# Queries and keys by seven half-size products instead of eight, with the message products moved

## The chip, the cores and the metric

The kernel runs on one core of a Trainium2 chip. The metric is the device time of one execution in microseconds (us), given as the median over the executions of a run. Engines: PE is TensorE's matmuls, PEld its weight loads, DVE is VectorE, ACT is ScalarE, POOL is GpSimd.

## The reference, cut to what matters

Two graph-attention layers on 64 graphs of 256 nodes with 512 features, all in fp32. The part concerned is in layer 0:

```python
m = embs @ map_w.T + map_b                       # 256 x 512 per graph
...
q = (m @ q_w.T + q_b)                            # 256 x 512, 8 heads of 64
k = (m @ k_w.T + k_b)
scores = einsum('bhsd,bhtd->bhst', q, k) / sqrt(64)
...
sem_h = (embs @ gcn_map_w.T + gcn_map_b)         # the "messages"
Ax = einsum('hbst,hbtd->hbsd', adj_h, sem_h)
```

(... cut: normalization, cosine threshold, softmax, layer 1.)

## The kernel before

Each graph goes through a software pipeline, one *period* per graph, in which layer 0 of graph i, layer 1 of graph i-1 and the preparation of graphs i+1 and i+2 are interleaved by hand. The order in the program is the order of each engine's queue; TensorE's timelines below show its products in that order.

```python
def features_first(wt, src, ms, name):
    p = bank(name)                                # one PSUM bank of a ring of 8
    nk = wt.shape[1]                              # 4 chunks of 128
    for n, m in enumerate(ms):
        for c in range(nk):
            nc.tensor.matmul(p[:, n, :], wt[:, c, m * P:(m + 1) * P], src[:, c, :],   # 128 x 256
                             start=(c == 0), stop=(c == nk - 1))
    return p

def queries(g, n):                                # keys: the same with wk, bk, kT
    ...
    p = features_first(w.wq, g.mT, (2 * n, 2 * n + 1), f"p_q{g.i}_{n}")
    for k in range(2):
        m = 2 * n + k
        nc.scalar.activation(g.qT[:, m, :], p[:, k, :], AF.Identity, bias=w.bq[:, m:m + 1])

def messages(g, t):
    ...
    for c in range(NKC):
        nc.tensor.matmul(p, g.hT[:, c, t * P:(t + 1) * P], w.wc[:, c, :], ...)          # 128 x 512
    nc.vector.tensor_add(g.sem[:, t, :], p, w.bc)

def period(i):                                    # g: graph i, b: i-1, nx: i+1, n2: i+2
    ...                                           # scores of g, mapped(nx), cosines, layer-1 scores of b
    if g:
        far_off(g, 2, co[2])                      # VectorE: a <- co, e; GpSimd: e + a, halves
        far_off(g, 3, co[3])
    if nx:
        messages(nx, 0)
        messages(nx, 1)
    if n2:
        edges(n2)
        moments(n2, f"0_{n2.i}")
    if nx:
        queries(nx, 0)
        queries(nx, 1)
    ...                                           # values, sums, division, result 0 of b, heads_back(g)
    if nx:
        lengths(nx, p_n)
        keys(nx, 0)
    ...                                           # moments, deviations, normalized of g (layer 1)
    if nx:
        ...
        keys(nx, 1)
    if g:
        hT = turned(g, f"1_{i}")                  # p_t: waits for VectorE's xn
    ...
```

## Time and profile before

| what | before |
|---|---|
| time, median | 4105.03 us (4103.81 to 4105.85, 4 runs) |
| one period (steady, from the starts of p_m) | 63.05 or 63.06 us, 60 times of 61 |
| TensorE busy / clock granted (share of full clock) | 99% / 0.998 |
| queries + keys per graph, start to next start | 7.00 + 6.94 = 13.94 us |
| messages per graph | 6.97 us |

Lines of a profile group instructions by program line, engine, operation and tile. These two are the heaviest users of the weight loader in the change (busy us, mean ns of one, then the idle time before them and what ended it):

```profile
L191 PE MATMUL p_q<-mT,wq 128*128 128x256 f32 x2048 | 452.7, 379 | 0.0
L191 PEld LDWEIGHTS p_q<-mT,wq 128*128 128x128 f32 x2048 | 389.0, 190 | 80.1 <-issue 30.5
```

An fp32 matmul leaves two records, so 64 graphs x 16 matmuls are 2048. The matmuls never waited (0.0). The 379 ns are a record's latency, not its pitch; the pitch is 7.00/32 = 0.219 us (0.216 from record to record, and 0.309 once, from the last one to av, whose tiles are 128*64 and not 128*128), and the loads run beside the matmuls: 31 of the 32 loads of queries lie in the 6.67 us from 2027.79, inside the 7.00 us of their matmuls.

### The profile page before, as it was taken

The page shows a single profiled execution, that of the slowest core. Times are in us where ns is not written, and L with a number is a line of the kernel's source. Part 1 is how long each engine was busy: PE and PEld are TensorE (multiplying, and loading weights), DVE is VectorE, ACT ScalarE, POOL GpSimd, SP SyncE. Part 2 cuts the span into 40 slices and gives each one's busy share as a digit, 9 for nine tenths or more (in the row PEclk, how much of TensorE's full clock was granted, in tenths as well). Part 3 has the DMA queues.
Part 4 walks back from the last instruction along what each step waited for, and adds up shares of the span by engine and source line. Part 5 has one row for each costly group of instructions (what it writes and reads, how often), then busy time and mean ns, then how long its engine had stood idle before and what let it go on. Part 6 is the DMA issues. An engine that isn't in the chain of part 4 may idle for free.

```text
span 4102.0 us, 56638 instructions
## 1 busy us (share of the span) xinstructions
PE 4050.7 (99%) x23649; PEld 3072.0 (75%) x23649; DVE 2233.5 (54%) x3160; ACT 1453.2 (35%) x3010; POOL 1559.9 (38%) x1030
## 2 busy tenths in 40 slices
PE   8999999999999999999999999999999999999997
PEld 6777777777777777777777777777777777777775
DVE  3555555555555555555555555555555555555553
ACT  2333333333333333333333333333333333333332
POOL 2334344243343343443433434434334344343341
PEclk9999999999999999999999999999999999999999
DMA  2000000000000000000000000000000000000000
GB/s 88 12 23 12 23 23 12 22 13 22 23 12 23 23 12 23 15 19 23 12 23 22 12 23 17 18 23 12 22 23 12 23 17 18 23 12 23 23 6 17
DMA packets 56517, 81.59 MB, mean 20 GB/s; under 512 B 21888, under 2 KB 21888, under 8 KB 56256
## 3 DMA queue, kind: packets, MB, share of 16 engines
q1 hardware_dynamic: 52224, 71.32, 5.3%
q0 software_dynamic: 1760, 6.55, 0.4%
q8 instruction: 188, 3.08, 0.3%
q14 instruction: 73, 0.60, 0.0%
q10 hardware_dynamic: 2272, 0.04, 0.0%
HBM read 44.34 MB, written 33.55 MB: 19 GB/s over the span
## 4 chain that ended last, share of the span: by engine, by line
PE 91%; DVE 6%; ACT 1%; issue 0%; DMA 0%; POOL 0%; ACTq 0%; POOLq 0%; DVEq 0%
PE p_q L191 16%; PE p_k L191 16%; PE p_m L191 11%; PE p_s L231 11%; PE sc L280 8%; PE p_o L389 6%; PE co L280 6%; PE p_v L476 5%; DVE rz L382 5%; PE av L308 3%; PE p_t L181 3%; PE p_b L251 2%; PE zb L375 1%; PE p_l L356 1%; DVE oT L384 1%; ACT z L378 1%
## 5 line engine op out<-in xcount | busy, mean ns | idle before, releaser
L315 POOL TENSOR_TENSOR e<-e,a 128x1024 f32<-128x1024 f32 x252 | 654.7, 2598 | 1649.9 <-DVE a L295 1649.9
L288 DVE TENSOR_TENSOR e<-e,mask 128x1024 f32<-128x1024 f32 x384 | 563.8, 1523 | 164.6 <-ACT e L287 164.6
L301 POOL TENSOR_TENSOR d<-e 128x512 f32<-128x512 f32 x378 | 528.7, 1413 | 42.9 <-DVE e L288 23.1
L255 DVE TENSOR_TENSOR nT<-mT,p_b 128x512 f32<-128x512 f32 x128 | 82.2, 684 | 713.3 <-PE p_b L251 713.3
L191 PE MATMUL p_m<-hT,wm 128*128 128x256 f32 x2048 | 461.0, 383 | 0.7 <-ACT hT L182 0.7
L231 PE MATMUL p_s<-wc,hT 128*128 128x512 f32 x1024 | 456.5, 599 | 0.0
L191 PE MATMUL p_k<-mT,wk 128*128 128x256 f32 x2048 | 452.8, 379 | 0.0
L191 PE MATMUL p_q<-mT,wq 128*128 128x256 f32 x2048 | 452.7, 379 | 0.0
L191 PEld LDWEIGHTS p_q<-mT,wq 128*128 128x128 f32 x2048 | 389.0, 190 | 80.1 <-issue 30.5
L191 PEld LDWEIGHTS p_m<-hT,wm 128*128 128x128 f32 x2048 | 385.2, 191 | 72.1 <-ACT e L287 20.5
L382 DVE RECIPROCAL rz<-z 128x512 f32<-128x512 f32 x64 | 214.6, 3353 | 406.1 <-ACT z L378 406.1
L191 PEld LDWEIGHTS p_k<-mT,wk 128*128 128x128 f32 x2048 | 384.2, 190 | 49.6
L287 ACT ACTIVATE e<-sc 128x512 f32<-128x512 f32 x768 | 389.7, 617 | 84.6 <-PE sc L280 83.9
L263 ACT ACTIVATE qT<-p_q,bq 128x256 f32<-128x256 f32 x256 | 107.5, 470 | 867.6 <-PE p_q L191 867.6
L360 POOL TENSOR_TENSOR xs<-xs,o 128x512 f32<-128x512 f32 x128 | 159.8, 1270 | 580.1 <-DVE o L358 580.1
L231 PEld LDWEIGHTS p_s<-wc,hT 128*128 128x128 f32 x1024 | 189.3, 190 | 235.2 <-issue 234.5
L295 DVE SCALAR_TENSOR_TENSOR a<-co,e 128x512 f32<-128x512 f32 x512 | 317.0, 679 | 11.4 <-PE co L280 11.4
L389 PE MATMUL p_o<-wo,oT 128*128 128x512 f32 x512 | 248.3, 608 | 15.4 <-DVE oT L384 15.3
L463 POOL TENSOR_TENSOR xs<-xs,bo_b 128x512 f32<-128x512 f32 x128 | 170.6, 1351 | 222.8 <-DVE xn L172 219.1
L280 PE MATMUL co<-nT 64*128 64x256 f32 x2048 | 251.4, 384 | 1.2 <-DVE a L295 1.2
L476 PEld LDWEIGHTS p_v<-wv,hT 128*128 128x128 f32 x1024 | 194.5, 190 | 54.1 <-ACT hT L182 15.5
L476 PE MATMUL p_v<-wv,hT 128*128 128x256 f32 x1024 | 231.6, 379 | 0.4 <-ACT hT L182 0.4
(113 smaller groups left out, 5443.8 us busy)
## 6 DMA issues: line engine op xcount, KB each, us to landing
xs<-in_x_dram SPq DMA_DIRECT2D x64, 512.0 KB, 3.8
out_dram<-xs SPq DMA_DIRECT2D x64, 512.0 KB, 2.8
ad<-in_adj_dram SPq DMA_DIRECT2D x64, 64.0 KB, 3.6
wm<-in_L_gnn_map_w_dram POOLq DMA_DIRECT2D x1, 1024.0 KB, 9.1
gw<-in_L_gnn_gcn_map_w_dram POOLq DMA_DIRECT2D x2, 512.0 KB, 10.0
wq<-in_L_gnn_q_w_dram POOLq DMA_DIRECT2D x1, 1024.0 KB, 13.8
wk<-in_L_gnn_k_w_dram POOLq DMA_DIRECT2D x1, 1024.0 KB, 16.4
wv<-in_L_gnn_Wv_dram POOLq DMA_DIRECT2D x1, 512.0 KB, 18.0
```

Of the source, the lines that this page charges most:

```text
L191: nc.tensor.matmul(p[:, n, :], wt[:, c, m * P:(m + 1) * P], src[:, c, :], start=(c == 0), stop=(c == nk - 1))
L231: nc.tensor.matmul(p, g.hT[:, c, t * P:(t + 1) * P], w.wc[:, c, :], start=(c == 0), stop=(c == NKC - 1))
L280: nc.tensor.matmul(ps[s][:, j, :], rows[h, c, j * P:(j + 1) * P], cols[h, c, :], start=True, stop=True)
L287: nc.scalar.activation(e[:, s, :], p.rearrange("p j q -> p (j q)"), AF.Exp, scale=SCALE)
L288: nc.vector.tensor_mul(e, e, mask[:, None, :].to_broadcast([P, 2, NT * S]))
L295: nc.vector.scalar_tensor_tensor(q[:, s, :], p.rearrange("p j q -> p (j q)"), THRESHOLD, e[:, s, :], op0=ALU.is_gt, op1=ALU.mult)
L301: nc.gpsimd.tensor_add(d, e[:, :, :S], e[:, :, S:])
L315: nc.gpsimd.tensor_add(g.e[c], g.e[c], g.q[c])
L382: nc.vector.reciprocal(rz, b.z)
L389: nc.tensor.matmul(p, b.oT[:, c, t * P:(t + 1) * P], w.wo1[:, c, :], start=(c == 0), stop=(c == NIC - 1))
L463: nc.gpsimd.tensor_add(g.xs[:, t, :], g.xs[:, t, :], w.bo_b)
L476: nc.tensor.matmul(p[:, t, :], hT[:, c, t * P:(t + 1) * P], w.wv1[:, c, :], start=(c == 0), stop=(c == NKC - 1))
```

## The change

The intent: Strassen's identity (in Winograd's form with shared sums) computes a product of 2x2 blocks by seven block products instead of eight. The blocks are 256 x 256 of weights and 256 features x 128 tokens of mT, so the products run in 128-column matmuls. Sums of mT blocks are made by GpSimd, the weight blocks once at the start. The products accumulate in PSUM where the identity allows. The message products go behind the sums, into the places that the keys had. To make room, several tiles lose their second buffer.

```diff
+    def left_factors(src, name):
+        a = [src[:, HC * k:HC * (k + 1), t * P:(t + 1) * P] for t in range(2) for k in range(2)]
+        ss = sb1.tile([P, 4, HC, P], F32, tag="wide", name=f"ss{name}")
+        nc.gpsimd.tensor_add(ss[:, 0], a[2], a[3])
+        nc.gpsimd.tensor_sub(ss[:, 1], ss[:, 0], a[0])
+        nc.gpsimd.tensor_sub(ss[:, 2], a[0], a[2])
+        nc.gpsimd.tensor_sub(ss[:, 3], a[1], ss[:, 1])
...
+    def seven_products(left, wt, bias, dst, name):
+        pa = bank(f"{name}_a", [P, 2, HC, P])          # two halves of one bank
+        pb = bank(f"{name}_b", [P, 2, HC, P])
+        pc = bank(f"{name}_c", [P, HC, P])
...                                                     # product(): 4 matmuls of 128 columns; biased(): 2 ScalarE copies
+        product("a", pa[:, 0], 1, a12)
+        p2 = biased(pa[:, 0], 0, 2, bufs=1)
+        product("a", pa[:, 1], 0, a11)
+        out(0, 0, pa[:, 1], p2)                        # VectorE
+        yield
+        product("c", pc, 6, a22)
+        p4 = biased(pc, 0, 4)
+        yield
+        product("b", pb[:, 0], 3, s1)
+        p5 = biased(pb[:, 0], 1, 5)
+        product("b", pb[:, 1], 2, s4)
+        yield
+        product("a", pa[:, 1], 4, s2)
+        u4 = sb1.tile([P, HC, P], F32, tag="uu", name=f"uu{name}")
+        nc.vector.tensor_add(u4, pa[:, 1], p5)
+        out(0, 1, pb[:, 1], u4)
+        yield
+        product("a", pa[:, 1], 5, s3)
+        out(1, 1, pa[:, 1], p5)
+        out(1, 0, pa[:, 1], p4)
...
+    def queries_and_keys(g):
+        ...
+        for step in (q, k, q, q, k, q, k, k, q, k):
+            next(step, None)
...
         if nx:
-            messages(nx, 0)
-            messages(nx, 1)
+            queries_and_keys(nx)
         if n2:
             edges(n2)
             moments(n2, f"0_{n2.i}")
-        if nx:
-            queries(nx, 0)
-            queries(nx, 1)
...
             lengths(nx, p_n)
-            keys(nx, 0)
+            messages(nx, 0)
...
-            keys(nx, 1)
+            messages(nx, 1)
```

(Cut: the loading of four weight blocks and the making of seven, eight VectorE subtractions at the start; tiles hT, sem, rn, adb from two buffers to one, xn from four to two; the sums and the tile avs, which share one place; the messages of the first graph, now ahead of its products; the slow path for unusual inputs, which does not run here.)

Names used below: P1 and P2 are the products of weight blocks 0 and 1, the first to be issued; p_q_a, p_q_b, p_q_c are q's three PSUM banks and p_k_a to p_k_c those of k; u2, u4, u5 are ScalarE's copies of products with the bias added. A *turn inside a bank* is: a product into one half of a bank, ScalarE's copy out of that half, the next product into the other half.

## The prediction

> **What bounds the kernel now.** I read the page first (busy shares, the chain that ended last), then one period of the tensor engine's timeline, then the vector engine's timeline in the same stretch.
>
> ```profile
> PE 4050.7 (99%) x23649; PEld 3072.0 (75%) x23649; DVE 2233.5 (54%) x3160; ACT 1453.2 (35%) x3010; POOL 1559.9 (38%) x1030
> ...
> PE 91%; DVE 6%; ACT 1%; issue 0%; DMA 0%; POOL 0%; ACTq 0%; POOLq 0%; DVEq 0%
> ```
>
> TensorE is busy 99% and is 91% of the chain: it issues almost without a gap, so a microsecond saved there is a microsecond saved, and any new gap there is added in full. The timeline of TensorE shows a period of 63.05 us per graph (the query matmuls start at 1964.73 and again at 2027.78), 64 graphs in all. The parts that the change touches:
>
> ```profile
> 2018.99 1.89 PE L280 MATMUL co<-nT 64*128 64x256 f32 x16
> 2020.81 7.13 PE L231 MATMUL p_s<-wc,hT 128*128 128x512 f32 x16
> 2027.78 7.07 PE L191 MATMUL p_q<-mT,wq 128*128 128x256 f32 x32
> 2034.78 1.95 PE L308 MATMUL av<-e,v 128*64 128x256 f32 x16
> ...
> 2042.65 1.96 PE L389 MATMUL p_o<-wo,oT 128*128 128x512 f32 x4 [0.17 <-DVE oT L384]
> ...
> 2045.75 7.07 PE L191 MATMUL p_k<-mT,wk 128*128 128x256 f32 x32
> 2052.69 1.07 PE L181 MATMUL p_t<-ident,xn 128*128 128x128 f32 x8
> ```
>
> Columns: start, length, engine and line, operation, count. One fp32 matmul leaves two records. From start to next start queries take 7.00 us and keys 6.94 us, 0.216 us per record of 256 columns: 13.94 us per graph. Messages (p_s) take 6.97. No bracket on p_s, p_q, p_k: they wait for nothing. What the other engines do behind them:
>
> ```profile
> 2019.44 4.24 DVE L288 TENSOR_TENSOR e<-e,mask 128x1024 f32<-128x1024 f32 x2 [0.36 <-ACT e L287]
> ...
> 2023.60 2.47 DVE L295 SCALAR_TENSOR_TENSOR a<-co,e 128x512 f32<-128x512 f32 x4
> 2026.00 0.68 DVE L232 TENSOR_TENSOR sem<-p_s,bc 128x512 f32<-128x512 f32 x1
> ```
>
> VectorE is behind: TensorE left the cosine products (co) at 2020.81, VectorE finishes with them at 2026.0, 5.2 us later. Now this costs nothing, because messages and queries ask VectorE for nothing in that time.
>
> The price of a half-width record stands at the start of the run, where weights are folded by 128-column fp32 matmuls:
>
> ```profile
> L108 PEld LDWEIGHTS p_wc<-gt,gw x32: 192/192/192, 27.8 to 31.2; 128*128 128x128 f32 x32
> L108 PE MATMUL p_wc<-gt,gw x32: 275/275/275, 27.9 to 31.4; 128*128 128x128 f32 x32
> ```
>
> The timeline puts 32 loads in 3.65 us with the last one's 0.19: (3.65-0.19)/31 = 0.112 us per record.
>
> [...] the masking of e takes 1.16 us each at 2008.29 (4.63 for 4, GpSimd idle) and 2.12 at 2019.44 (GpSimd busy).
>
> **The change part by part.**
>
> 1. Matmul work. Seven products of 2x2 blocks, 28 matmuls of 128 columns instead of 16 of 256, for q and for k: 112 records x 0.112 = 12.5 us instead of 13.94. Saved: 1.4 us per graph, 92 us in all, 2.2%. The arithmetic fell by an eighth, weight loads rose from 64 to 112, and the records got 4% dearer per column. This is the whole possible gain.
>
> 2. Turns inside a bank. I read the built program's waits engine by engine. Three times per graph the order on TensorE is: product into half of a bank; ScalarE copies that half out with bias (two 128x128 instructions); the very next product goes to the other half of the same bank and waits for that copy. This is so for P2 then P1 of q, and for blocks 3 then 2 of q and of k. Nothing stands between. One turn: a record lasts 275 ns at a pitch of 112, so 0.16 until it has ended; 0.04 to ScalarE's start (p_q ended 2034.85, its copy began 2034.89); two copies,[...] 0.63; 0.1 back to TensorE (oT ended 2042.50, p_o began 2042.65); 0.1 for the exposed load of the first record (377 against 275 ns in p_bc). Together 1.0 us, three times: +3.0.
>
> 3. The fourth turn, P2 then P1 of k, is worse. ScalarE's copy of k's P2 has a single buffer (u2) with q's, so it first waits until VectorE has added q's P1 and P2; and that add stands on VectorE after all four a<-co pairs, which end 5.2 us after TensorE starts on q. From there: add 0.42 (as rn<-p_n, 0.41), 0.04, copies 0.63, back 0.1: TensorE can go on at 6.4. It reaches this wait after three products of 0.89, one turn of 1.0 and 0.1 for the change of array tiling: 3.8. Stall +2.6. The four GpSimd operations of the left factors (about 0.73 each, half of 128x512's 1.27 to 1.41 plus its fixed part, 2.9 us from 2016.4) stand before e<-e,a and push it to 2019.3, where VectorE's masking wants to begin;[...] VectorE ends 0.5 to 1.6 us later. I take +0.9, so +3.5.
>
> 4. Later products: those that accumulate into a region that VectorE has read (blocks 4 and 5) have one or two products of 0.89 between, against about 0.65 for the read and its two hand-overs: no stall. VectorE's ten adds per graph, 4.2 us, are otherwise beside TensorE.
>
> 5. Messages in place of keys fill 6.97 instead of 6.94: nothing. But their evacuation moves from ScalarE to VectorE's queue, ahead of the statistics for layer 1. p_s of token tile 0 ends about 3.7 us after p_l, VectorE's add 4.4, statistics 1.9 more, square root, reciprocal, first xn at about 7.5; TensorE arrives at 7.0. Now p_t waits 0.1 on average. +0.4.
>
> 6. p_o stays as it is: z, rz, oT shift with TensorE, and the statistics of graph n+2 are done before z. Single buffers for hT, sem, rn, adb and two for xn: each next writer comes after the last reader in TensorE's own order, no wait. Seven weight blocks at the start, 8 subtractions and longer first products: +4 us once.
>
> Sum per graph: -1.4 +0.1 +3.0 +3.5 +0.4 = +5.6, less a little where the turns overlap; I take +5.4. 63 x 5.4 + 4 = 344; 4105 + 344 = 4449, rounded to 4445 us.
>
> **The rivals.** (a) The gain comes through: if the waits inside a bank were already met when TensorE comes there, 4105 - 92 + 25 (p_t) = 4040 us. For it: the author interleaved q and k in order to hide the turns. Against it: three turns have no product between, and the order of the queues is fixed. (b) Only the short turns count, because VectorE is less late than I think: -1.4 + 0.1 + 4.0 + 0.4 = +3.1, about 4305. Against it: the 5.2 us of lag stand alike at 1957.76, 2020.81 and in the next period. (c) GpSimd becomes a drag: left factors plus contention delay VectorE by the full 1.6 or more, +6.3 and over, 4510. (d) Weight loads become the bound and a record costs more than 0.112: each 0.01 more is 1.1 us per graph, 70 us.
>
> **Range and chances.** The turns are certain in kind; their size (0.8 to 1.2) moves the total by 25 either way, VectorE's lag at the fourth turn by 60, p_t by 25, the record pitch by 20. Range 4345 to 4530. Faster by over 2% needs (a) in full, 3%; within 2% 4%; slower 93%.
>
> **What the profile after would show.** TensorE's busy share falls to about 92% or less (busy time nearly as now or lower), with idle before the product line put down to ScalarE, three times about 1 us and once about 3 us per graph; that one preceded by ScalarE waiting for VectorE. Record pitch in the products near 0.112. Masking of e on VectorE as slow as now or slower. A small idle before p_t put down to VectorE's xn. A period of about 68.5 us. I am wrong if TensorE has no gaps in the products, or if the long gap is missing, or if a large new gap stands at p_o.

Of the sum, two stand without their reasons: in part 2 the 0.63 us of the two copies (0.16 + 0.04 + 0.63 + 0.1 + 0.1 = 1.03, taken as 1.0), and in part 3 the +0.9, with the 0.5 to 1.6 us behind it. The sum: -1.4 + 0.1 + 3.0 + 3.5 + 0.4 = +5.6 per graph, taken as +5.4; 63 x 5.4 + 4 = 344; 4105 + 344 = 4449, put as 4445 us. The changed kernel's trace has the copies at 0.63 us, the four sums on GpSimd at 0.73 each, and the +0.9 at 0.27 in most periods (below).

## The result

| | before | after |
|---|---|---|
| time, median | 4105.03 us (4 runs) | 4487.45 us (4468.53 to 4494.38, 4 runs) |
| ratio | 1 | 1.0925 (95%: 1.0891 to 1.0958) |
| period, most frequent | 63.06 us | 68.07 or 68.08 us |
| queries + keys | 13.94 us in two pieces | 18.68 us in one piece |
| clock granted | 0.998 | 0.988 (0.984 to 0.988 in four runs) |

A ratio is the mean time of one kernel's fast runs over that of the other's of the same rounds, so it is not quite the ratio of the medians. The change made the kernel 9% slower; the predicted 4445 us (4345 to 4530) was 42 us too low and its range holds. All outputs are right.

The page of the changed kernel, busy shares and the chain that ended last:

```profile
PE 4077.0 (91%) x26721; PEld 3157.7 (71%) x26721; DVE 2366.5 (53%) x3805; ACT 1486.0 (33%) x3266; POOL 1745.2 (39%) x1292
...
PE 73%; POOL 14%; DVE 7%; ACT 2%; issue 2%; POOLq 0%; DVEq 0%; ACTq 0%
```

TensorE is no longer 91% of the chain, and GpSimd stands in it with 14%. Its timeline in one ordinary period (start us, length us, what; in brackets the idle time before and who ended it):

```profile
2004.50 1.16 PE L238 MATMUL p_q_a<-mT,wq 128*128 128x128 f32 x8
2006.38 1.16 PE L238 MATMUL p_q_a<-mT,wq 128*128 128x128 f32 x8 [0.72 <-ACT u2p_q L247]
2007.37 1.06 PE L238 MATMUL p_k_a<-mT,wk 128*128 128x128 f32 x8
2011.14 1.16 PE L238 MATMUL p_k_a<-mT,wk 128*128 128x128 f32 x8 [2.71 <-ACT u2p_k L247]
2012.13 1.06 PE L238 MATMUL p_q_c<-mT,wq 128*128 128x128 f32 x8
2013.03 1.06 PE L238 MATMUL p_q_b<-ssq,wq 128*128 128x128 f32 x8
2014.89 1.13 PE L238 MATMUL p_q_b<-ssq,wq 128*128 128x128 f32 x8 [0.81 <-POOL d L373]
...
2019.42 1.16 PE L238 MATMUL p_k_b<-ssq,wk 128*128 128x128 f32 x8 [0.72 <-ACT u5p_k L247]
...
2023.18 1.95 PE L380 MATMUL av<-e,v 128*64 128x256 f32 x16
...
2041.39 1.06 PE L195 MATMUL p_t<-ident,xn 128*128 128x128 f32 x8 [0.27 <-DVE xn L186]
```

There are the four turns inside a bank: three short ones (0.72, 0.81, 0.72 us idle) and one long one (2.71), and a small new wait at p_t. The third bracket names GpSimd, but the same line at 431.69 us names ScalarE's u5p_q: that product waits for both, GpSimd's ss has long been written, and a bracket names whichever event came last. The chain's 14% for GpSimd rests on this and is no cause. Between the turns a product of 8 records has a pitch of 0.89 or 0.90 us, 0.112 per record. What the long turn waits for is on ScalarE's and VectorE's timelines in the same period:

```profile
2010.46 0.63 ACT L247 ACTIVATE u2p_k<-p_k_a,bk 128x128 f32<-128x128 f32 x2 [4.14 <-DVE qT L251]
```

```profile
2003.13 4.51 DVE L360 TENSOR_TENSOR e<-e,mask 128x1024 f32<-128x1024 f32 x2 [0.36 <-ACT e L359]
2007.56 2.47 DVE L367 SCALAR_TENSOR_TENSOR a<-co,e 128x512 f32<-128x512 f32 x4
2009.96 0.41 DVE L251 TENSOR_TENSOR qT<-p_q_a,u2p_q 128x256 f32<-128x256 f32 x1
```

ScalarE's copy of k's P2 could start only when VectorE had used the copy of q's P2 (2009.96 + 0.41), and VectorE came to that only after the masking and the cosine thresholds.

So far the period is 5.02 us longer, 61 x 5.02 = 306 us of the 365 that the profiled runs differ by. The rest: 34 us stand in 17 longer periods (69.4 to 71.6 us), 15.6 at the start of the run (6.9 before the first p_m, 8.7 in the first two periods), and the remaining 9 at its end, where the 64th graph's products stand. One of the longer periods:

```profile
426.58 2.08 PE L238 MATMUL p_k_a<-mT,wk 128*128 128x128 f32 x8 [2.71 <-ACT u2p_k L247]
428.46 1.53 PE L238 MATMUL p_q_c<-mT,wq 128*128 128x128 f32 x8
429.82 1.06 PE L238 MATMUL p_q_b<-ssq,wq 128*128 128x128 f32 x8
```

The product after the long gap has a pitch of 1.88 us for 8 records and not 0.99: the clock record there grants TensorE 0.5 of full clock for 3.413 us. The view by stretches gives a granted clock of 0.72 between 426.58 and 431.69. The trace's clock records show 19 such half-clock stretches (0.5 granted) of 3.413 or 6.827 us before the last 100 us of the run; before the change there is none there. One of the 19 follows a wait of 3.46 us at p_t in the second period, 18 follow the long gap. Their beginnings lie whole multiples of 3.413 us apart from each other (all 19 within 0.01 us of multiples of 3.41333), a grid that does not follow the periods (68.07 us are 19.94 steps). The prediction had none of this.

### The profile page after: what moved, and what is told of

The parts are those of the page before. It is cut to its first block, busy times and chain, and to the rows that moved or that the text cites. A ratio compares the mean times of both kernels' runs of the same rounds, so it can differ in the third digit from the quotient of the medians.

```text
span 4466.8 us, 64461 instructions
## 1 busy us (share of the span) xinstructions
PE 4077.0 (91%) x26721; PEld 3157.7 (71%) x26721; DVE 2366.5 (53%) x3805; ACT 1486.0 (33%) x3266; POOL 1745.2 (39%) x1292
## 4 chain that ended last, share of the span: by engine, by line
PE 73%; POOL 14%; DVE 7%; ACT 2%; issue 2%; POOLq 0%; DVEq 0%; ACTq 0%
PE p_m L205 10%; PE av L380 8%; POOL d L373 6%; POOL e L387 6%; PE p_o L461 5%; PE sc L352 5%; PE p_v L544 5%; PE p_k L205 5%; PE p_q L205 5%; PE p_s L311 5%; PE p_k_a L238 3%; PE p_k_b L238 3%; PE p_t L195 3%; PE p_q_a L238 3%; PE p_q_b L238 2%
## 5 line engine op out<-in xcount | busy, mean ns | idle before, releaser
L360 DVE TENSOR_TENSOR e<-e,mask 128x1024 f32<-128x1024 f32 x384 | 584.7, 1578 | 165.7 <-ACT e L359 165.7
L219 POOL TENSOR_TENSOR ssq<-mT 128x256 f32<-128x256 f32 x64 | 47.0, 734 | 1561.7 <-PE co L352 1549.1
L238 PE MATMUL p_k_a<-mT,wk 128*128 128x128 f32 x1024 | 156.0, 300 | 173.4 <-ACT u2p_k L247 173.4
L238 PEld LDWEIGHTS p_k_a<-mT,wk 128*128 128x128 f32 x1024 | 136.7, 208 | 185.6 <-ACT u2p_k L247 185.6
L461 PE MATMUL p_o<-wo,oT 128*128 128x512 f32 x512 | 247.7, 607 | 11.6 <-DVE oT L456 5.0
L352 PE MATMUL sc<-qT,kT 64*128 64x256 f32 x2048 | 233.0, 378 | 0.0
L380 PE MATMUL av<-a,sem 128*64 128x256 f32 x2048 | 231.9, 379 | 0.0
## 6 DMA issues: line engine op xcount, KB each, us to landing
wq<-in_L_gnn_q_w_dram POOLq DMA_DIRECT2D x4, 256.0 KB, 11.6
```

Of the source, the lines that this page charges most:

```text
L238: nc.tensor.matmul(region[:, f, :], wt[:, block, c, f * P:(f + 1) * P], src[:, c, :], start=p not in opened, stop=True, skip_group_check=True)
L352: nc.tensor.matmul(ps[s][:, j, :], rows[h, c, j * P:(j + 1) * P], cols[h, c, :], start=True, stop=True)
L360: nc.vector.tensor_mul(e, e, mask[:, None, :].to_broadcast([P, 2, NT * S]))
L380: nc.tensor.matmul(av[s * DH:(s + 1) * DH, n, :], vs[:, j, (h0 + s) * DH:(h0 + s + 1) * DH], q[:, s, j * S:(j + 1) * S], start=(j == 0), s ...
L461: nc.tensor.matmul(p, b.oT[:, c, t * P:(t + 1) * P], w.wo1[:, c, :], start=(c == 0), stop=(c == NIC - 1))
```

## The experiments

**Theory.** The four turns inside a bank, and the single buffer that ties the fourth one to VectorE's lag, cost the time; the arithmetic saving is real. **Rivals:** 128-column matmuls are too dear because of their weight loads; the move of the messages takes away a cover that VectorE needs; contention between GpSimd and VectorE. Later: the half clock is a consequence of the long gap.

### 1. No turns: both products of a bank before the copy

```diff
         product("a", pa[:, 0], 1, a12)
-        p2 = biased(pa[:, 0], 0, 2, bufs=1)
         product("a", pa[:, 1], 0, a11)
+        p2 = biased(pa[:, 0], 0, 2, bufs=1)
...
         product("b", pb[:, 0], 3, s1)
-        p5 = biased(pb[:, 0], 1, 5)
         product("b", pb[:, 1], 2, s4)
+        p5 = biased(pb[:, 0], 1, 5)
```

> Both products of a bank are issued before ScalarE copies one of them out (turns inside a bank gone, all else as in the changed kernel). Theory, turns: the seven-product stretch falls from 18.68 us to 112 records x 0.112 + 0.1 = 12.65 us, the period to about 62.1 us (63.05 - 13.94 + 12.65 + 0.27 at p_t), no half-clock stretches in mid-run, the time to about 4060 us (the start of the run costs some 15 us more than before). Rival, narrow records (128-column matmuls bound by weight loads cost far more than 0.112 us): the stretch stays above 16 us and the time above 4300 us. Rival, VectorE's lag is what counts and finds another wait: a new gap of 2 us or more at block 4 of q, time above 4200 us.

Measured: 4055.79 us (4054.96 to 4057.3), ratio to before 0.9883 (0.9866 to 0.9899). TensorE's timeline of the products:

```profile
2001.49 2.05 PE L238 MATMUL p_q_a<-mT,wq 128*128 128x128 f32 x16
2003.38 1.95 PE L238 MATMUL p_k_a<-mT,wk 128*128 128x128 f32 x16
2005.17 1.06 PE L238 MATMUL p_q_c<-mT,wq 128*128 128x128 f32 x8
2006.06 1.95 PE L238 MATMUL p_q_b<-ssq,wq 128*128 128x128 f32 x16
...
2014.20 1.95 PE L380 MATMUL av<-e,v 128*64 128x256 f32 x16
```

No bracket is left, and the stretch is 2014.20 - 2001.49 = 12.71 us. The period is 62.09 or 62.10 us in 41 of 61 cases, up to 62.15 in nearly all others, and one half-clock stretch remains before the last 100 us, at 63.5 us behind a wait of 3.46 us at p_t. VectorE's lag is still there: its two maskings take 4.5 us in 18 periods and 5.7 in 42, more than in the changed kernel. TensorE comes to the banks that VectorE reads only later, so nothing waits. Two lines of program order gave back 432 us, and the rivals of narrow matmuls and of the lag fall in the form stated.

### 2. A second buffer for the fourth turn alone

```diff
-        p2 = biased(pa[:, 0], 0, 2, bufs=1)
+        p2 = biased(pa[:, 0], 0, 2 if name.startswith("p_q") else "u", bufs=1)
```

(The copy of k's P2 goes into the tile "uu", which is free at that time.)

> The copy of k's second product gets a buffer of its own (it takes the place of the sum tile of k, same size); the turns stay. Theory: the long gap of 2.71 us before k's block 0 becomes a short one of 0.72 us like the others, period 68.07 - 2.0 = 66.1 us, and with no gap over 1 us the half-clock stretches go; time about 4305 us. Rival, contention of GpSimd and VectorE: the long gap stays, time above 4420 us.

Measured: 4310.13 us (4308.9 to 4310.6), ratio 1.05 (1.0483 to 1.0518). The long gap has become a fourth short one:

```profile
2002.60 1.16 PE L238 MATMUL p_k_a<-mT,wk 128*128 128x128 f32 x8 [0.71 <-ACT uup_k L247]
```

The period is 66.07 or 66.08 us in 59 of 61 cases, so the single buffer costs 68.07 - 66.08 = 1.99 us. One half-clock stretch is left before the last 100 us, at 66.8 us. Against experiment 1 it is 66.08 - 62.10 = 3.98 us for four short turns: 0.995 us each.

### 3. The second bank alone

Only the lower half of the diff of experiment 1.

> Only the second bank (blocks 3 and 2) issues both products before the copy; P2 and P1 stay as in the changed kernel. Theory: two short turns of about 0.9 to 1.0 us go, period about 66.2 us, the long gap of 2.7 us and some half-clock stretches stay; time about 4350 us. If the short turns cost nothing of their own: 4480 us.

Measured: 4387.31 us (4383.25 to 4393.64), ratio 1.0691 (1.0673 to 1.0709), 37 us above what was expected. The undisturbed period is 66.04 to 66.06 us in 16 cases, so the two turns are worth 68.07 - 66.06 = 2.01 us, as above. But in 37 periods it is 67.7 to 67.9 us and in eight 68.7 or 68.8: there the half clock follows the long gap, which is as long as in the changed kernel:

```profile
2034.70 1.77 PE L238 MATMUL p_k_a<-mT,wk 128*128 128x128 f32 x8 [2.71 <-ACT u2p_k L247]
```

There are 47 half-clock stretches before the last 100 us against 19, and the granted clock of the run is 0.979. The size of a turn was right; that the half clock strikes 45 periods of 61 here and 17 of 61 there was not foreseen (experiment 8 has the reason).

### 4. The move alone, on the kernel before

```diff
         if nx:
-            messages(nx, 0)
-            messages(nx, 1)
+            for n in range(2):
+                queries(nx, n)
+                keys(nx, n)
         if n2:
...
-        if nx:
-            queries(nx, 0)
-            queries(nx, 1)
...
-            keys(nx, 0)
+            messages(nx, 0)
...
-            keys(nx, 1)
+            messages(nx, 1)
```

> The kernel before with only the move: all eight-product queries and keys where the messages were, messages at the two places of the keys. Theory: only the wait at p_t comes, about 0.27 us per period, 4105 + 17 = 4122 us. Rival, the move is a main cost because messages no longer cover VectorE's lag: 4200 us or more.

Measured: 4131.18 us (4130.7 to 4133.05), ratio 1.0067 (1.005 to 1.0084). The period is 63.46 or 63.47, 0.41 us longer, against the expected 0.27. The wait at p_t is there as in the changed kernel, 0.27 or 0.28 us; the rest is 0.07 for queries with keys (14.01) and 0.07 for the messages (7.31 less the wait). The move costs 26 us; it is not the main cause.

### 5. The price of narrow matmuls alone, on the kernel before

```diff
     for n, m in enumerate(ms):
-        for c in range(nk):
-            nc.tensor.matmul(p[:, n, :], wt[:, c, m * P:(m + 1) * P], src[:, c, :], ...)
+        for t in range(NT):
+            for c in range(nk):
+                nc.tensor.matmul(p[:, n, t * P:(t + 1) * P], wt[:, c, m * P:(m + 1) * P],
+                                 src[:, c, t * P:(t + 1) * P], ...)
```

(In a copy of features_first that only the queries and keys of layer 0 use.)

> The kernel before with its eight-product queries and keys in 128-column matmuls (two for each of 256 columns; twice the weight loads, same arithmetic). Theory (a record of 128 columns costs 0.112 us[...], and nothing else): 128 x 0.112 + 0.1 = 14.4 us in place of 13.94, about 0.45 us per graph, 4105 + 29 = 4134 us. Rival, narrow matmuls cost the changed kernel its time: 4250 us or more.

Measured: 4131.93 us (4131.47 to 4133.42), ratio 1.0067 (1.0054 to 1.0081).

```profile
2042.30 7.31 PE L192 MATMUL p_q<-mT,wq 128*128 128x128 f32 x64
2049.54 1.95 PE L319 MATMUL av<-e,v 128*64 128x256 f32 x16
```

The 64 records take 2049.54 - 2042.30 = 7.24 us, 0.113 each, in place of 7.00 for 32 wide ones. Narrow records cost 0.42 us per period (63.47). Doubling the weight loads is cheap here (64 records with their 64 loads take 0.24 us more than 32), but it takes back some 30% of what the identity saves (an eighth of 13.94 is 1.74 us; 13.94 - 12.71 = 1.23 remain).

### 6. The message adds behind the normalization as well

On top of experiment 1, VectorE's adds of the messages are issued after layer 1's normalization.

```diff
             lengths(nx, p_n)
-            messages(nx, 0)
+            p_s = messages(nx, 0)          # matmuls only
...
             nc.vector.reciprocal(nx.rn, nx.rn)
-            messages(nx, 1)
+            message_out(nx, 0, p_s)        # VectorE's add
+            message_out(nx, 1, messages(nx, 1))
```

> Both copies late (as the run before without turns), and VectorE's add of the messages stands behind the normalization of layer 1. Theory: the wait of 0.27 us at p_t goes, 62.1 to 61.8 us per period, 4056 - 17 = 4039 us. Rival, the wait at p_t has another cause (statistics or square root late anyway): no change, 4056 us.

Measured: 4026.16 us (4025.39 to 4026.73), ratio 0.9809 (0.9795 to 0.9824). The messages and p_t on TensorE's timeline:

```profile
2010.92 7.03 PE L311 MATMUL p_s<-wc,hT 128*128 128x512 f32 x16
2017.79 1.04 PE L195 MATMUL p_t<-ident,xn 128*128 128x128 f32 x8
```

The bracket at p_t is gone, and from p_s to p_t it is 6.87 us, where experiment 1 has 2032.41 - 2025.10 = 7.31. The period is 61.63 us, 0.47 shorter, not 0.27: this wait cost TensorE more than the idle time in its bracket. A record of p_s lasts 0.59 us at a pitch of 0.43, so some 0.16 until the last one has ended comes on top (an estimate from these two figures). It makes 62 x 0.47 = 29 us, as measured.

### 7. The start of the run

In the changed kernel TensorE's first matmul is at 20.49 us, before the change at 13.56. GpSimd's queue issues six more weight loads, and in it they stand ahead of the conversion of the first graph's adjacency (adb), which the first transposes need. The conversion before and after the change:

```profile
12.88 0.62 POOL L199 CAST adb<-ad 128x512 bf16<-128x512 uint8 x1
```

```profile
19.81 0.62 POOL L278 CAST adb<-ad 128x512 bf16<-128x512 uint8 x1
```

It begins 6.93 us later, as the first matmul does. Each block load takes 0.72 us of GpSimd in the changed kernel, and there are eight in place of two. On top of experiment 6:

```diff
+        edges(graphs[0])
         w.load_rest()
         def first(n):
-            edges(graphs[n])
+            if n > 0:
+                edges(graphs[n])
```

> As the run with late adds, and GpSimd converts the first graph's adjacency before it issues the weight loads. Theory: the later start of the changed kernel (first matmul at 20.5 instead of 13.6 us) comes from GpSimd's queue, which issues six more weight loads first; with the conversion ahead of them the first matmul begins at 6 to 10 us: 4039 - 12 = 4027 us, periods unchanged. Rival, the start is set by the arrival of the weights: no gain, 4039 us.

Measured: 4014.80 us (4013.1 to 4016.41), ratio 0.9781 (0.9767 to 0.9796).

```profile
9.22 0.58 PE L287 MATMUL p_a<-ident_b,adb 128*128 128x128 bf16 x4 [9.22 <-DVE ident_b L46]
```

The first matmul is at 9.22 us and waits for VectorE now; periods are unchanged (61.63). This is the best version measured: 2.2% faster than the kernel before, and the only one whose whole interval lies beyond 2% (experiment 6 lies across it). It puts the conversion ahead of all the loads of load_rest and not of the six alone, so it gains more than the change had lost.

### 8. The long gap filled with useless work

The changed kernel, all waits as they are, with two products whose result is overwritten later, issued in the long gap:

```diff
         p2 = biased(pa[:, 0], 0, 2, bufs=1)
+        if name.startswith("p_k"):
+            for n in range(2):
+                ...                        # 4 matmuls of 128 columns into q's bank c, overwritten afterwards
```

> The changed kernel with two useless products (16 records, 1.8 us, their result is overwritten) in the long gap before k's block 0; nothing waits less. Theory of the clock: the half-clock stretches come from the gap of 2.7 us; with the gap filled to under 1 us they go, while the wait ends at the same time: every period about 68.07 us, no half-clock stretch in mid-run, time 4468 - 33 = 4436 us, in place of 4468 to 4494. Rival, the half clock has nothing to do with the gap: 4470 us or more, with half-clock stretches.

Measured: 4444.92 us (4443.31 to 4446.63), ratio 1.0829 (1.0811 to 1.0847). With 1024 more matmul records in the run (27,745), the kernel is 4487.45 - 4444.92 = 43 us faster by the medians than without them. The end of the wait is where it was:

```profile
2001.23 1.16 PE L240 MATMUL p_k_a<-mT,wk 128*128 128x128 f32 x8 [0.93 <-ACT u2p_k L249]
```

The idle time is 0.93 us in place of 2.71, the period 68.07 to 68.09 us in 51 of 61 cases, and 3 half-clock stretches are left before the last 100 us in place of 19; the runs lie within 3.3 us of each other instead of 26. The eight longer periods that remain (six of 69.2 us, two of 70.8) leave a gap of 2.06 us beside the filling, 1.13 more than the others; in the changed kernel the three periods with maskings of 5.65 us have 1.15 more (3.86 for 2.71). So the half clock of these runs comes from the long gap (19 stretches with it, 3 with it filled), and with it the scatter of the changed kernel's times.

Why it strikes only some periods can be read from the traces: cut each long gap at the lines of the 3.413 us grid on which the run's stretches begin. In the changed kernel the half clock begins at the end of a grid step that held at least 1.97 us of the gap (18 of 18 gaps), and never where the largest piece was 1.96 us or less (44 of 44). In experiment 3 the limit lies between 1.89 us (16 of 16 without) and 1.91 us (46 of 46 with). Here the two gaps of 2.06 us that lie within one step have it, the six whose largest piece is at most 1.76 us have not. So in these runs a gap of 2.71 us passed unpunished when a grid line fell near its middle (largest piece 1.36 to 1.96 us in the changed kernel), and where it fell was up to the period: 18 of 62 gaps were struck in the changed kernel, 46 of 62 in experiment 3.

## Why the prediction was right, point by point

- **The possible gain.** Part 1 said 12.5 us plus 0.1 for the change of tiling instead of 13.94. Measured 12.71 (experiment 1); the record pitch of 0.112, read from the weight folding at the start, held in the run (0.89 to 0.90 per 8) and in experiment 5 (0.113). Worth 1.23 us per period, not 1.4.
- **The short turns.** Part 2 said 1.0 us each; measured 0.995 (experiment 2 less experiment 1). Two ScalarE copies take 0.63 us, as the sum had them (0.364 for one of 128 columns; one of 256 columns took 0.470 before).
- **The long turn.** The order of things was as described: ScalarE waits for VectorE's add, which stands behind the thresholds. The size was 1.99 + 0.995 = 2.99 us, not 3.5: of the two terms, the wait itself (+2.6) measures 2.72, and the one for GpSimd's left factors (+0.9) was too large, 0.27. In 58 of 62 periods the pair of maskings took 4.51 us, 0.27 above the 4.24 before, and GpSimd's e<-e,a beside it 3.40 to 3.43; only in three periods, where GpSimd's e<-e,a took 2.36 us, as it does where no masking runs beside it (2.34 to 2.36), was it 5.65, a gap of 3.86 us. I had averaged two cases that are not equally frequent. This is one of the three, on VectorE's and on GpSimd's timeline:

```profile
1725.92 5.65 DVE L360 TENSOR_TENSOR e<-e,mask 128x1024 f32<-128x1024 f32 x2 [0.36 <-ACT e L359]
```

```profile
1725.93 2.36 POOL L387 TENSOR_TENSOR e<-e,a 128x1024 f32<-128x1024 f32 x1
```

- **p_t.** Part 5 said +0.4; the move alone measures +0.41 (experiment 4), of which the bracket is 0.27, and experiment 6 takes 0.47 away.
- **p_o and the single buffers** stayed as said: p_o's idle time of 15.4 us in all went to 11.6, and no new wait of another kind stands in the period.
- **The sum.** 5.4 us per period was said, 5.02 measured: 5.02 = -1.23 + 3 x 0.995 + 2.99 + 0.33 (p_s to p_t, 7.30 for 6.97) - 0.06 (p_n to p_o, 0.72 for 0.78).
- **Missed: the half clock.** No step of the prediction had it. It is most of the 34 us in longer periods of the profiled run. The other three runs take 16 to 26 us more at a lower clock (0.984 to 0.986); they have no trace, but the clock points to the same.
- **The start, right in sum.** The prediction has 4 us once and 5.4 for each of the first two periods, 14.8 in all; 15.6 were measured. But the 6.9 before the first p_m were not its VectorE subtractions and longer products: GpSimd issues the weight loads ahead of work that TensorE waits for (experiment 7).
- **Partly luck: the total.** The steady periods were forecast 23 us too high (61 x 0.38), and the half clock and the end of the run, neither of which was in the sum, filled this up and went beyond it. Experiment 8, at 4445 us nearly without half clock, meets the predicted number by chance: six of its periods are longer for another reason.
- **Of the rivals,** (a), the whole gain, is what the idea gives when the turns are taken out (4056, without the move's wait 4026). (b), (c) and (d) were refuted by the 2.71 us gap, by the 4.51 us maskings and by the pitch.

What stays open: no run moved the long gap along the 3.413 us grid on purpose, and why the limit is 1.89 to 1.91 us in one run and 1.96 to 1.97 in the other is not shown. It is a limit for the long gaps alone: the wait of 3.46 us at p_t in the changed kernel was struck with at most 1.80 us of it in one step.

## What to carry to other kernels

When a matmul saves arithmetic by more, smaller products, price each product's hand-over before its flops: here a product that waited for a copy out of the other half of its PSUM bank cost TensorE 0.995 us, which is more than the product itself (0.89). Issue all products of a bank first and the reads after them, and look in the built program for waits between neighbours on the busiest engine. An idle gap on the busiest engine can cost more than its length: in the changed kernel each of the 18 long gaps with at least 1.97 us inside one step of 3.413 us was followed by a step at half clock (clock record 0.5), and none of the 44 with 1.96 us or less was. A copy tile with one buffer hands one engine's lag to another that had nothing to do with it (1.99 us per period here).
